# A two-layer vision network on one core: the layer-0 selective scan on 16 states x 8 channels, and attention with scores one key block ahead

## The chip, the cores and the metric

The kernel runs on one core of one Trainium2 chip. The metric is the device time of one execution in microseconds (us). Before the change it is 17,470.7 us, the median of three runs (17,456.07, 17,470.7 and 17,522.3).

The engines are named as in the profile: PE does the matrix products and loads their weights (PEld), DVE is the vector engine, ACT the scalar engine (activation functions), POOL the third elementwise engine; SP issues the transfers (DMA). SBUF is the on-chip memory, PSUM the accumulators that PE writes.

## The reference

Two images of 96 channels x 96 x 96 pass through two layers. Each layer adds a mixer to the image and then a two-layer feed-forward block (FFN), both after a normalisation over the channels.

The mixer of layer 0 projects to 192 channels, computes an offset per pixel, samples the image bilinearly there, and cuts the result into windows of 6 x 6 tokens. In each window it runs four selective scans (rows, columns, and both backwards; index kg), each over 192 channels with 16 states:

```python
def step(hst, inputs):
    ut, dt, bt, ct = inputs
    dA = jnp.exp(dt[..., None] * A)
    hst = hst * dA + (dt * ut)[..., None] * bt[:, :, None, :]
    y = jnp.einsum('bkdn,bkn->bkd', hst, ct)
    return (hst, y)
```

Here dt is the softplus of a projection, and B and C (bt, ct) are projections of the samples. The four results are added, normalised, gated and projected back to 96 channels.

The mixer of layer 1 is an attention of three heads with 32 channels each. Keys and values are the 9,216 pixels, queries are 2,304 cells, means of 2 x 2 pixels:

```python
attn = jnp.einsum('bhdn,bhdm->bhnm', k, q_samp) * scale
attn = jax.nn.softmax(attn, axis=-2)
distribution = jnp.einsum('bhdn,bhnm->bhdm', v, attn)
```

The distribution is then spread to the pixels with a local 3 x 3 softmax, a 5 x 5 depthwise convolution of the values is added, and the sum is projected.

## The kernel before, in words

**Layer 0** (`_layer0`, L581) goes through 32 stripes of 6 rows, that is 16 windows or 576 tokens each (T = 576, H2 = 288). For each stripe there is a front (`_l0_front`), a scan and a back (`_l0_back`).

The front normalises, projects (pi and pz), runs the 3 x 3 convolution pc on PE (L356), makes the offsets fr (L391), samples on POOL (L404 to L421), and then computes, for four directions and two halves of the channels, dl = softplus (eight units, L466 to L493) and du = dl times the samples xs. ACT, DVE and POOL each have a part of a unit: Abs, Relu, Exp and Ln on ACT, e on DVE (L485), the sums r, w and the product du on POOL (L488 to L491). dl and du are written to DRAM. At the places where a window begins, dl is set to 1e33, so that its decay becomes zero.

The scan puts 4 states x 32 channels into the 128 partitions. A section is one direction and one half of the channels. Per section, `load_section` brings dl and du from DRAM, each read four times over (864 KB each, the four copies leading). Per state group i of four, `decay` brings the row of C that is needed (cre, 288 KB) and computes dA = exp(A dl) on ACT (L636). Then there are two token halves, so 64 steps u a stripe:

- `b_rows` (L652): PE spreads the rows of B over the partitions by a product with a selection matrix, into PSUM (pB).
- `scan` (L668): DVE multiplies du by pB and puts the product bp into PSUM; L679: DVE scans h = dA h + bp over 864 columns, into SBUF; L680: POOL multiplies h by C.
- `states` (L694), three steps later: three products with 32 output columns each fold the states of h into py.

`collect` (L721 for one of the two cases) adds py to Y on DVE. The back normalises Y, gates and projects it and runs the FFN.

The order of the work is written out by hand: front and back are generators, whose `yield` states a price. Between two scan steps the loop takes generator steps of the back of the stripe before and of the front of the stripe after, until the sum of the prices has reached its share of `k.between` = 205. `_in_order` then fixes this order on PE, DVE, ACT and POOL.

**Layer 1** has, for each image: a normalisation stage; then `_l1_attention`; then the rows (`_l1_rows`) with the FFN. `_l1_attention` makes vT, kH and qH, then runs a max pass (L845, L852) that finds the maximum per query and head, so that it can be subtracted. Then comes the value pass: six chunks of 384 cells, and in each 72 key blocks of 128 pixels:

- scores sc: per head one bf16 product (L881) that puts in the negated maximum, and one fp32 product (L890);
- pr = exp(sc), one ACT instruction on 128 x 1152 (L898);
- values av (L900): four products with 33 output columns, two of 384 cells (heads 0 and 1, in one accumulator) and two of 192 cells (the halves of head 2, in another). The 33rd column of vT is one, so its row is the denominator.

The scheduler keeps the order of the code on PE: scores of a block, its values, scores of the next. At the end of a chunk, for each of the four parts, the denominator row is spread by a product (pb, L912), its reciprocal taken (L920) and multiplied in.

`_ln` (L77) is the normalisation that the nrm stage and all FFNs use: it takes the inverse square root with Ln and Exp on ACT (L97, L98).

Of the kernel before, what the change touches and what calls it, by code (L numbers as in the profile page):

```python
# [15 lines left out]
ENGINES = (  # L16
    mybir.EngineType.PE,
    mybir.EngineType.DVE,
    mybir.EngineType.Activation,
    mybir.EngineType.Pool,  # L20
)
# [3 lines left out]
NB = 2  # L25
# [10 lines left out]
NQ = 4  # L36
CB = 32
NBL = C // CB
PAST = 1e33
NG = 12  # L40
HID = 384
# [13 lines left out]
def _in_order(k, tc, start):  # L55

    last = {}
    for i in k.nc.cur_bb.bb.instructions[start:]:
        if i.engine in ENGINES:
            if i.engine in last:  # L60
                tc.add_manual_dep(
                    i,
                    last[i.engine].name,
                    mybir.DependencyInfo(
                        mybir.DependencyClass.NoSync, mybir.DependencyReason.DATA
                    ),
                    reason="in_order",
                )
            last[i.engine] = i


def _all(steps):
    for _ in steps:
        pass


def _ln(k, pool, psum, ptag, x, eps, out, pre, tags=None, bufs=None):  # L77
# [3 lines left out]
    t0, t1 = tags or (pre + "xc", pre + "sq")  # L81
# [3 lines left out]
    yield 1.3  # L85
    xc = pool.tile([C, 2, n], F32, tag=t0, name=pre + "xc", bufs=bufs)
    nc.vector.tensor_tensor(xc, x, mu[:C, :2, :n], ALU.subtract)
    sq = pool.tile([C, 2, n], F32, tag=t1, name=pre + "sq", bufs=bufs)
    nc.scalar.activation(sq, xc, AF.Square)
    yield 0.8  # L90
# [3 lines left out]
    yield 1.3  # L94

    rs = sq
    nc.scalar.activation(rs, va[:C, :2, :n], AF.Ln, bias=eps[:C])  # L97
    nc.scalar.activation(rs, rs, AF.Exp, scale=-0.5)  # L98
    yield 1.6
    kw = {"saturate": False} if out.dtype == F8 else {}  # L100
    nc.vector.tensor_tensor(out, xc, rs, ALU.mult, **kw)
    yield 0.7


def _ffn(k, pool, psum, ptag, w, x1, out, tags=None, bufs=None):
# [4 lines left out]
    yield from _ln(k, pool, psum, ptag, x1v, k.eps5, xq, "f", tags, bufs)  # L110
    h16 = pool.tile([128, NM, T], HP, tag="fh16", name="fh16")
    h8 = pool.tile([128, NM, T], F8, tag="fh8", name="fh8")
    for m in range(NM):
# [6 lines left out]
        yield 1.3  # L120
        nc.vector.tensor_scalar(
            h16[:, m, :], h16[:, m, :], w.b1[:, m : m + 1], 0.0, ALU.add, ALU.max
        )
    nc.vector.tensor_copy(h8, h16, saturate=False)
    yield 1
# [12 lines left out]
    yield 1.4  # L138
    nc.vector.tensor_scalar(y16, y16, w.b2, None, ALU.add)
    nc.vector.tensor_tensor(out, x1, y16, ALU.add)  # L140
    yield 0.9
# [28 lines left out]
def _l0_weights(k, a, cp, tmp, ps, dram):  # L170
# [33 lines left out]

    xp = tmp.tile([C, 2, KG, 6 + 2 * NS], F32, tag="xp", name="xp")
# [5 lines left out]
    k.w_bc = cp.tile([C, 2, 2, 3, 2, NS], F32, tag="w_bc", name="w_bc")  # L211
    for kg in range(KG):
        o, kk = kg % 2, kg // 2
        nc.vector.tensor_copy(k.w_dl[:, :, o, kk * 6 : kk * 6 + 6], xp[:, :, kg, 0:6])
        nc.sync.dma_start(k.w_dt[kk * 6 : kk * 6 + 6, kg, :], a["dt_w"][kg])
        for j in range(3):
            src = xp[:, :, kg, 6 : 6 + NS] if j < 2 else xp[:, :, kg, 6 + NS :]
            nc.vector.tensor_copy(k.w_bc[:, :, o, j, kk, :], src)


    k.selb = cp.tile([2 * CB, 2, NQ, 128], F32, tag="selb", name="selb")
    for j in range(2):
        rows = slice(CB * j, CB * j + CB)
        for kk in range(2):
            c0 = CB * j + NS * kk
            for i in range(NQ):
                nc.vector.tensor_copy(
                    k.selb[rows, kk, i].rearrange("p (q c) -> p q c", c=CB),
                    k.ident[rows, c0 + i : c0 + NS : NQ].unsqueeze(2).to_broadcast([CB, NQ, CB]),
                )  # L230


    k.fold = cp.tile([128, CB], F32, tag="fold", name="fold")
    nc.vector.tensor_reduce(
        k.fold, k.ident.rearrange("p (q c) -> p c q", c=CB), AX.X, ALU.add
    )

    ad = dram.tile([NS, KG * 2, C], F32, tag="ad", name="ad")
    src = a["A_logs"].rearrange("(n d) (k g) -> n d k g", n=NS, g=NG)
    for n in range(NS):
        nc.sync.dma_start(ad[n].rearrange("k (d g) -> d k g", g=NG), src[n])
    na = KG * 2 * NBL
    at = tmp.tile([NQ * na, 128], F32, tag="at", name="at")
    rows = ad.rearrange("(q i) k (b c) -> i (k b) q c", i=NQ, c=CB)
    for i in range(NQ):
        nc.sync.dma_start(
            at[i * na : (i + 1) * na, :].rearrange("p (q c) -> p q c", c=CB), rows[i]  # L250
        )
    pa = ps.tile([128, 128], F32, tag="pa", name="pa")
    nc.tensor.transpose(pa[:, : NQ * na], at, k.ident[: NQ * na, : NQ * na])
    k.A = cp.tile([128, NQ, KG, 2, NBL], F32, tag="A", name="A")
    Af = k.A.rearrange("p i k h b -> p (i k h b)")
    nc.scalar.activation(Af, pa[:, : NQ * na], AF.Exp)
    nc.vector.tensor_scalar(Af, Af, -1.0, -1e-30, ALU.mult, ALU.min)
# [9 lines left out]

def _l0_front(k, P, f, x, b, s):


    nc = k.nc
    r0 = WIN * s - 1
    lo, hi = max(r0, 0), min(r0 + 8, HW)
    temp = lambda shape, name: P.front.tile(shape, F32, tag="g", name=name, bufs=5)
    half2 = lambda v: v.rearrange("p (c n) -> p c n", c=2)


    xt = temp([C, 8, HW], "xt")
    if lo > r0:
        nc.gpsimd.memset(xt[:, 0, :], 0.0)  # L280
    if hi < r0 + 8:
        nc.gpsimd.memset(xt[:, 7, :], 0.0)
    nc.sync.dma_start(xt[:, lo - r0 : hi - r0, :], x[b, :, lo:hi, :])
    xin = P.front.tile([C, 2, 8, HW + 2], F32, tag="xin", name="xin")
    nc.gpsimd.memset(xin[:, :, :, 0 : HW + 2 : HW + 1], 0.0)
    yield 0.3

    halves = lambda v: v.rearrange("p (c r) w -> p c (r w)", c=2)
    mu = P.ps.tile(k.pshape, F32, tag="p", name="amu")
    for c in range(2):  # L290
        nc.tensor.matmul(mu[:C, c, :384], k.mean96, halves(xt)[:, c, :], start=True, stop=True)
    yield 1.7
    xc = temp([C, 2, 384], "axc")
    nc.vector.tensor_tensor(xc, halves(xt), mu[:C, :, :384], ALU.subtract)
    rs = temp([C, 2, 384], "ars")
    nc.scalar.activation(rs, xc, AF.Square)
    yield 1
    va = P.ps.tile(k.pshape, F32, tag="p", name="ava")
    for c in range(2):
        nc.tensor.matmul(va[:C, c, :384], k.mean96, rs[:, c, :], start=True, stop=True)  # L300
    yield 1.7
    nc.scalar.activation(rs, va[:C, :, :384], AF.Ln, bias=k.eps6[:C])
    nc.scalar.activation(rs, rs, AF.Exp, scale=-0.5)
    yield 1.8
    xn = temp([C, 8, HW], "xn")
    nc.gpsimd.tensor_tensor(halves(xn), xc, rs, ALU.mult)
    yield 1.7

    for half in range(2):
# [9 lines left out]
        yield 1.7  # L319
# [5 lines left out]
        yield 1  # L325
# [3 lines left out]
    for half in range(2):  # L329
# [9 lines left out]
        yield 1.3  # L339
# [5 lines left out]
        yield 1  # L345


    t = temp([C, 2, T], "t")
    for oh in range(2):
        pc = P.ps.tile(k.pshape, F32, tag="p", name="pc")  # L350
        n = 0
        for ih in range(2):
            for tap in range(9):
# [10 lines left out]
                yield 1.3  # L364
        nc.scalar.activation(  # L365
            half2(t[:, oh]),
# [5 lines left out]
        yield 0.8  # L372

    fr = temp([C, 2, WIN, HW], "fr")
    for yx in range(2):
# [10 lines left out]
        yield 2.6  # L386
# [3 lines left out]
        yield 0.8  # L390
    nc.vector.tensor_scalar(fr, fr, 0.5, 0.5, ALU.mult, ALU.add)  # L391
    yield 0.7

    xs0 = P.hand.tile([C, 2, T], F32, tag="xs0", name="xs0")
    xs1 = P.front.tile([C, 2, T], F32, tag="xs1", name="xs1")
    f.xs0 = xs0
    dif = temp([C, 2, 7, HW], "dif")
    top = temp([C, 2, WIN, HW], "top")
# [104 lines left out]
def _l0_back(k, P, f, ffn, res, dst):  # L503
# [74 lines left out]
    yield 0.1  # L578


def _layer0(k, tc, a, x, x2d):  # L581


    nc = k.nc
# [600 lines left out]
```

## Time and profile before

| | |
|---|---|
| profiled execution, its own time | 17,470.7 us |
| its span in the trace | 17,468.9 us |
| layer 0 | 0 to 10,720 us |
| image 1: normalisation, max pass, value pass, rows | 160, 644, 1,544, 971 us |
| image 2: normalisation, max pass, value pass, rows | 212, 639, 1,572, 1,007 us |
| busy over the span | PE 75%, DVE 55%, POOL 37%, ACT 36% |
| DMA | 929.26 MB, mean 53 GB/s |

The stages follow one another. Boundaries are read from the first and last instruction of each line; the first stage of image 1 begins at 10,720 us. In the profile a group of instructions is named by its line, its engine, what it writes and reads, and its size. A figure with x is a count. A trailing bracket is the time that the engine sat idle before the instruction, and who released it. Busy times do not tell by themselves what limits a stage: an engine that is idle may be waited for by nobody.

### The profile page before, as it was taken

How to read it: one execution, taken by the hardware profiler on the slowest of the kernel's cores; microseconds unless marked ns; L12 is line 12 of the kernel's file. 1: busy time of each engine (PE TensorE's matmuls, PEld its weight loads, DVE VectorE, ACT ScalarE, POOL GpSimd, SP SyncE). 2: the span in 40 equal slices, each digit the busy share in tenths (PEclk: the TensorE clock that was granted, in tenths of full speed). 3: DMA queues.
4: the chain of work that ended last, by engine and by line, in shares of the span. 5: the costliest groups of instructions: out<-in, count | busy, mean ns of one | idle time of the engine just before them, and what ended most of it. 6: DMA issues, size and time to landing. Idle time of an engine off the chain costs nothing.

```text
span 17468.9 us, 139858 instructions
## 1 busy us (share of the span) xinstructions
PE 13074.9 (75%) x52851; PEld 5578.3 (32%) x52851; DVE 9543.8 (55%) x7721; ACT 6238.1 (36%) x7697; POOL 6501.1 (37%) x4039
## 2 busy tenths in 40 slices
PE   6777777777777778777777776976668579766774
PEld 2233223223223223223223222222227332222463
DVE  3766666666666666666666665830006558000255
ACT  3444544544544444444444443013331120233211
POOL 4655655655655655655655652000001200000012
PEclk6556556556556556556556555579895555899756
DMA  1222222222222222222222221000000000000000
GB/s 59 93 84 80 91 86 81 89 88 81 87 88 81 86 91 80 84 94 80 84 93 80 83 91 48 0 1 1 1 3 7 8 10 0 1 1 1 3 8 7
DMA packets 292536, 929.26 MB, mean 53 GB/s; under 512 B 26300, under 2 KB 27060, under 8 KB 291764
## 3 DMA queue, kind: packets, MB, share of 16 engines
q1 hardware_dynamic: 291860, 920.31, 16.0%
q8 instruction: 416, 6.82, 0.2%
q14 instruction: 260, 2.13, 0.0%
HBM read 788.04 MB, written 132.17 MB: 53 GB/s over the span
## 4 chain that ended last, share of the span: by engine, by line
PE 48%; ACT 16%; DVE 12%; POOL 11%; issue 7%; DMA 5%; SPq 0%; ACTq 0%; POOLq 0%; DVEq 0%
PE pc L356 7%; PE pm L845 7%; PE av L900 6%; ACT pr L898 6%; PE pB L652 5%; PE sc L890 5%; PE py L694 4%; DVE h L679 4%; DMA cre<-c_d 4%; POOL h L680 3%; DVE acc L990 2%; ACT dA L636 2%; POOL acc L1018 2%; DVE bp L668 2%; PE lg L954 2%
## 5 line engine op out<-in xcount | busy, mean ns | idle before, releaser
L680 POOL TENSOR_TENSOR h<-h,cre 128x864 f32<-128x864 f32 x2048 | 4117.0, 2022 | 4136.9 <-DVE h L679 1502.6
L679 DVE TENSOR_TENSOR_SCAN h<-dA,bp 128x864 f32<-128x864 f32 x2048 | 4001.3, 1954 | 227.1 <-DVE bp L668 7.0
L668 DVE TENSOR_TENSOR bp<-dur,pB 128x864 f32<-128x864 f32 x2048 | 2169.9, 1060 | 2121.8 <-PE pB L652 1997.5
L636 ACT ACTIVATE dA<-dlr,A 128x576 f32<-128x576 f32 x3072 | 2154.3, 764 | 2590.0 <-DVE h L679 1800.9
L652 PE MATMUL pB<-bc,selb 32*128 32x288 f32 x4096 | 2440.7, 692 | 583.2 <-DVE bp L668 582.6
L694 PE MATMUL py<-h,fold 128*32 128x288 f32 x12288 | 2190.5, 627 | 771.1 <-DVE Y L721 339.9
L898 ACT ACTIVATE pr<-sc 128x1152 f32<-128x1152 f32 x864 | 976.4, 1130 | 3372.1 <-PE sc L890 3372.1
L900 PE MATMUL av<-pr,vT 128*33 128x384 f32 (+1 forms) x6912 | 1101.0, 443 | 940.7 <-ACT pr L898 940.7
L970 POOL MEMSET vch<- 96x1600 f32 x16 | 22.8, 1426 | 4482.7 <-PE av L900 2247.8
L652 PEld LDWEIGHTS pB<-bc,selb 32*128 32x128 f32 x4096 | 922.4, 279 | 2164.6 <-DVE bp L668 1092.8
L356 PE MATMUL pc<-xin,off 96*96 96x288 f32 x4608 | 1456.4, 472 | 95.1 <-ACT t L365 70.8
L920 DVE RECIPROCAL den<-pb 32x384 f32<-32x384 f32 (+1 forms) x48 | 93.6, 1951 | 2524.0 <-PE pb L912 2522.8
L845 PE MATMUL pm<-kH,qH 32*128 32x512 f32 x3888 | 1245.1, 1102 | 22.8 <-DVE m L852 21.3
L852 DVE TENSOR_REDUCE m<-pm 128x3 f32<-128x1536 f32 x648 | 1136.0, 1758 | 226.4 <-PE pm L845 204.3
L694 PEld LDWEIGHTS py<-h,fold 128*32 128x32 f32 x12288 | 381.4, 133 | 2158.5 <-issue 1370.8
L356 PEld LDWEIGHTS pc<-xin,off 96*96 96x96 f32 x4608 | 826.8, 188 | 734.1 <-issue 359.2
L1018 POOL TENSOR_TENSOR acc<-acc,ft 96x576 f32<-96x576 f32 x288 | 414.7, 1442 | 1474.6 <-DVE acc L990 1455.7
L890 PE MATMUL sc<-qH,kH 32*128 32x384 f32 x5184 | 946.9, 543 | 0.0
L900 PEld LDWEIGHTS av<-pr,vT 128*33 128x33 f32 x6912 | 347.5, 116 | 1862.3 <-ACT pr L898 1457.6
L1000 PE MATMUL pb<-ident,p 96*96 96x96 f32 x3456 | 415.7, 290 | 408.8 <-DVE ft L1010 394.0
L485 DVE SCALAR_TENSOR_TENSOR e<-dl,e 96x576 f32<-96x576 f32 x256 | 321.7, 1256 | 652.4 <-ACT dl L483 646.4
L845 PEld LDWEIGHTS pm<-kH,qH 32*128 32x128 f32 x3888 | 320.9, 298 | 945.0 <-DVE m L852 941.9
(201 smaller groups left out, 14182.9 us busy)
## 6 DMA issues: line engine op xcount, KB each, us to landing
cre<-c_d SPq DMA_DIRECT2D x1024, 288.0 KB
dlr<-dl_d SPq DMA_DIRECT2D x256, 864.0 KB
dur<-du_d SPq DMA_DIRECT2D x256, 864.0 KB
du_d<-du SPq DMA_DIRECT2D x384, 144.0 KB
dl_d<-dl SPq DMA_DIRECT2D x384, 144.0 KB
xt<-in_x SPq DMA_DIRECT2D x28, 288.0 KB
xr<-in_x SPq DMA_DIRECT2D x32, 216.0 KB
x2d<-x SPq DMA_DIRECT2D x32, 216.0 KB
```

Source lines behind the costliest of these rows:

```text
L356: nc.tensor.matmul(pc[:C, c, :H2], k.w_c1[:, ih, tap, oh * C : (oh + 1) * C], xin[:, ih, 3 * c + dy : 3 * c + dy + 3, dx : dx + HW], start ...
L636: nc.scalar.activation(dA[:, :, blk, :], rep[s][0][:, blk, :].rearrange("p (c n) -> p c n", c=2), AF.Exp, scale=k.A[:, i, o + 2 * kk, h, b ...
L652: nc.tensor.matmul(pB[:, :H2], k.selb[rows, kk, i, :], F[n].bc[o][rows, c * H2 : (c + 1) * H2], start=True, stop=True,)
L668: nc.vector.tensor_tensor(bv.rearrange("p (b n) -> p b n", b=NBL), rep[s][1][:, :, toks], brp.pop(u)[:, :H2].unsqueeze(1).to_broadcast([12 ...
L679: nc.vector.tensor_tensor_scan(hv, dv, bv, 0.0, ALU.mult, ALU.add)
L680: nc.gpsimd.tensor_tensor(h, h, cre[j][:, toks].unsqueeze(1).to_broadcast([128, NBL, H2]), ALU.mult)
L694: nc.tensor.matmul(P.py[CB * blk : CB * blk + CB, c, :H2], k.fold, ht[:, blk, :], start=(kk == 0 and i == 0), stop=(kk == 1 and i == NQ - 1),)
L845: nc.tensor.matmul(pm[:, hd, :], qH[hs, m * 128 : (m + 1) * 128], kH[hs, g * 512 : (g + 1) * 512], start=True, stop=True,)
L852: nc.vector.tensor_reduce(m18[:, :, g], pm, AX.X, ALU.max)
L890: nc.tensor.matmul(sc[:, hd, :384], kH[hs, n * 128 : (n + 1) * 128], qH[hs, cells], start=False, stop=True,)
L898: nc.scalar.activation(pr, sc[:, :, :384], AF.Exp, scale=HD**-0.5)
L900: nc.tensor.matmul(av[i][row : row + HD + 1, : hi - lo], vT[:, n, hd, :], pr[:, hd, lo:hi], start=(n == 0), stop=(n == nblk - 1),)
```

## The change

It has two parts that do not depend on each other, and one small thing that both share.

**Layer 0.** The 128 partitions hold 16 states x 8 channels. One step takes three groups of channels and all tokens, 128 x 1728. There are 32 steps a stripe. B and C are spread over the partitions by products with widened weights (pb), once per direction, and copied to SBUF (bc). dl and du are read from DRAM for every step, with 16 copies leading. dA is computed in place of the loaded dl, the product du B in place of the loaded du, the scan in the same place, the product with C too. A memset puts zero into dA where a window begins. Six products with a selection matrix (k.sel) fold a step into py. The sampling and the sums of the softplus are on DVE; r, w and e have one buffer each. Generators, prices and `_in_order` are gone from layer 0: the code calls scan, next front and back in turn, and the scheduler decides.

**Attention.** `scores` is called for the next block ahead of the values of the present one, also across chunks. pr has four buffers. The values of the three heads are three products with 32 output columns into one accumulator. The denominators are summed on DVE over the blocks (sums, 128 x 1152) and folded by three products at the end of a chunk, with one reciprocal. `_in_order` holds PE to this order.

**Shared.** `_ln` uses Sqrt on ACT and a reciprocal on DVE.

```diff
 def _ln(...)
...
-    nc.scalar.activation(rs, va[:C, :2, :n], AF.Ln, bias=eps[:C])
-    nc.scalar.activation(rs, rs, AF.Exp, scale=-0.5)
+    nc.scalar.activation(rs, va[:C, :2, :n], AF.Sqrt, bias=eps[:C])
+    nc.vector.reciprocal(rs, rs)
...
 def _l0_front(...)
...
-    g = nc.gpsimd
-    for half in range(2):
-        v = xin[:, half, 1:8, 1 : HW + 1]
-        g.tensor_tensor(dif[:, half], xin[:, half, 1:8, 2 : HW + 2], v, ALU.subtract)
...
+    nc.vector.tensor_tensor(dif, xin[:, :, 1:8, 2 : HW + 2], v, ALU.subtract)
+    nc.vector.tensor_tensor(top, dif[:, :, 0:6], fx, ALU.mult)
...
+                nc.scalar.activation(e, pt[:C, :, :H2], AF.Abs, bias=bias)
+                nc.scalar.activation(e, e, AF.Exp, scale=-1.0)
+                nc.vector.tensor_scalar(r, pt[:C, :, :H2], bias, 0.0, ALU.add, ALU.max)
+                nc.vector.tensor_scalar(w, e, 1.0, None, ALU.add)
+                nc.vector.scalar_tensor_tensor(e, w, 1.0, e, ALU.subtract, ALU.subtract)
+                nc.scalar.activation(w, w, AF.Ln)
+                nc.vector.tensor_tensor(w, w, e, ALU.subtract)
+                nc.vector.tensor_tensor(
+                    dl[:, half].rearrange("p (c n) -> p c n", c=2), w, r, ALU.add
+                )
+            nc.vector.tensor_tensor(du, dl, f.xs[o], ALU.mult)
...
+def _l0_scan(k, P, f):
...
+                for g0 in range(0, NG, U):
+                    dA = P.rep.tile([128, U, T], F32, tag="dA", name="dA", bufs=3)
+                    h = P.rep.tile([128, U, T], F32, tag="h", name="h", bufs=4)
+                    nc.sync.dma_start(
+                        dA.rearrange("p g t -> p (g t)"), _repeated(f.dl[kg], half, g0)
+                    )
+                    nc.sync.dma_start(
+                        h.rearrange("p g t -> p (g t)"), _repeated(f.du[kg], half, g0)
+                    )
+                    for g in range(U):
+                        i = (kg * 2 + half) * NG + g0 + g
+                        nc.scalar.activation(dA[:, g], dA[:, g], AF.Exp, scale=k.A[:, i : i + 1])
+
+                    first = 0 if kk == 0 else SEQ - 1
+                    nc.vector.memset(
+                        dA.rearrange("p g (w t) -> p (g w) t", t=SEQ)[:, :, first], 0.0
+                    )
+                    nc.vector.tensor_tensor(
+                        h, h, bc[kk][:, 0].unsqueeze(1).to_broadcast([128, U, T]), ALU.mult
+                    )
...
+                    nc.vector.tensor_tensor_scan(d1, d0, d1, 0.0, ALU.mult, ALU.add)
+                    nc.gpsimd.tensor_tensor(
+                        h, h, bc[kk][:, 1].unsqueeze(1).to_broadcast([128, U, T]), ALU.mult
+                    )
+                    for g in range(U):
+                        for c in range(2):
+                            nc.tensor.matmul(
+                                py[:C, c, :H2],
+                                k.sel[:, 11 - g0 - g : 11 - g0 - g + C],
+                                h[:, g, c * H2 : (c + 1) * H2],
...
 def _layer0(...)
...
+        ready = _l0_front(k, P, x, *stripes[0])
+        for n, (b, s) in enumerate(stripes):
+            f = ready
+            Y = _l0_scan(k, P, f)
+            if n + 1 < len(stripes):
+                ready = _l0_front(k, P, x, *stripes[n + 1])
+            _l0_back(k, P, f, Y, ffn, x2d[b, :, s * T : (s + 1) * T])
...
 def _l1_attention(...)
...
+        ahead = scores(0, 0)
         for mc in range(6):
...
+            av = pa.tile([128, 512], F32, tag="a", name="av")
+            sums = wk.tile([128, 3, 384], F32, tag="sums", name="sums", bufs=2)
             for n in range(nblk):
+                pr = ahead
+                if n + 1 < nblk:
+                    ahead = scores(mc, n + 1)
+                elif mc < 5:
+                    ahead = scores(mc + 1, 0)
                 for hd in range(HEADS):
                     nc.tensor.matmul(
+                        av[hd * HD : (hd + 1) * HD, :384],
                         vT[:, n, hd, :],
+                        pr[:, hd, :],
...
+                if n == 0:
+                    nc.vector.tensor_copy(sums, pr)
+                else:
+                    nc.vector.tensor_tensor(sums, sums, pr, ALU.add)
...
+        _in_order(k, tc, start, (mybir.EngineType.PE,))
```

## The prediction

> **What bounds the kernel now.** I read the page's totals first, then a table of stretches, then single lines and the order of time inside two stretches.
>
> ```profile
> PE 13074.9 (75%) x52851; PEld 5578.3 (32%) x52851; DVE 9543.8 (55%) x7721; ACT 6238.1 (36%) x7697; POOL 6501.1 (37%) x4039
> ```
>
> No engine is full over the whole span, so the stages must be read apart. Columns: stretch, its length, busy us of PE, PE weight load, DVE, ACT, POOL, then granted clock, DMA share, GB/s.
>
> ```profile
> 0.00:10720.00 10720.00, 8166.98 (x25733) 3191.14 (x25733) 7017.65 (x5140) 4799.05 (x6206) 6055.27 (x3729) 0.60 0.26 84
> 10880.00:11524.00 644.00, 625.65 (x1957) 161.90 (x1956) 570.79 (x344) 2.46 (x3) 0.00 (x0) 0.53 0.00 0
> 11524.00:13068.00 1544.00, 1043.96 (x7382) 397.33 (x7380) 48.01 (x40) 496.25 (x453) 0.00 (x0) 0.91 0.00 1
> 14890.00:16462.00 1572.00, 1069.26 (x7419) 407.46 (x7419) 60.09 (x52) 497.96 (x457) 1.43 (x1) 0.90 0.00 1
> ```
>
> Layer 0 is the first row: 10,720 of 17,469 us, PE 76% and DVE 65% busy. The last two rows are the value passes of the two images (the second row is a max pass, which the change leaves alone). In them PE is 68% and ACT 32% busy: 100% together, so they take turns. Instruction by instruction (start, length):
>
> ```profile
> 12391.86 1.17 PE L900 MATMUL av<-pr,vT 128*33 128x384 f32 x8 [1.11 <-ACT pr L898]
> 12392.95 0.58 PE L890 MATMUL sc<-qH,kH 32*128 32x384 f32 x1
> 12393.96 1.13 ACT L898 ACTIVATE pr<-sc 128x1152 f32<-128x1152 f32 x1 [2.15 <-PE sc L890]
> 12395.14 1.17 PE L900 MATMUL av<-pr,vT 128*33 128x384 f32 x8 [1.11 <-ACT pr L898]
> ```
>
> One key block is 12391.86 to 12395.14 = 3.28 us: value products 1.09, scores 1.0, exp 1.13, in series.
>
> In layer 0 the price of the scan matters. Its two DVE instructions (lowest/median/highest ns):
>
> ```profile
> L679 DVE TENSOR_TENSOR_SCAN h<-dA,bp x2048: 1952/1954/1956, 225.6 to 10670.9; 128x864 f32<-128x864 f32 x187
> L668 DVE TENSOR_TENSOR bp<-dur,pB x2048: 1045/1062/1064, 224.5 to 10669.7; 128x864 f32<-128x864 f32 x187
> ```
>
> First to last scan is 10,445 us for 32 stripes: 326.4 us each. Each of these two reads one input from PSUM, and neither ever gets longer, though POOL works beside them all the time. An operation with two SBUF inputs does (DVE, then POOL in the same microseconds):
>
> ```profile
> 5125.00 2.00 DVE L485 SCALAR_TENSOR_TENSOR e<-dl,e 96x576 f32<-96x576 f32 x1 [1.04 <-ACT dl L483]
> 5126.93 1.05 DVE L668 TENSOR_TENSOR bp<-dur,pB 128x864 f32<-128x864 f32 x1
> ```
> ```profile
> 5124.37 2.01 POOL L680 TENSOR_TENSOR h<-h,cre 128x864 f32<-128x864 f32 x1
> 5126.34 1.93 POOL L491 TENSOR_TENSOR du<-dl,xs 96x576 f32<-96x576 f32 x1
> ```
>
> L485 takes 0.73 us at its lowest; here it ends 0.62 after POOL's multiply ends at 5126.38. POOL's next, elsewhere 1.40, ends 1.27 after L485 does. They run one at a time, with about 0.13 us of start-up hidden at each handover.
>
> [...] while the 4-copy loads run alone (3115 to 3120 us) the share is 0.25 at 80 GB/s. [...]
>
> **The change, part 1: layer 0.** Per stripe 64 steps (multiply, scan, POOL multiply on 864 columns) become 32 on 1728. The states in partitions go from 4 to 16, so B no longer needs the 128 selection matmuls a stripe; multiply and scan now read both inputs from SBUF.
>
> Each loop step: [...] scan: 1954 ns for 864 is 2.08 ns per column beside 0.155 fixed, so 3.75; POOL multiply: 1.40 at 576 and 2.02 at 864 give 2.15 ns per column, so 3.88; a small memset 0.1. If the lock holds for whole instructions: 1.96 + 3.75 + 3.88 - 2 x 0.13 + 0.1 = 9.4 us. 32 steps are 300 us. DVE alone would be 5.8 (the bound below), and if the scan doesn't lock but the multiply does it is about 5.9. What else is there per step: ACT three exps of 0.76 = 2.3; PE 6 fold matmuls, 3 us at the rate of 0.5 each; DMA two loads of 864 KB, now 16 copies leading, thus all engines, at the 250 GB/s seen in the fullest stretches 7.1 us. All lie beneath 9.4.
>
> The hand interleave is gone. In the built order of the changed kernel, DVE has only the start of the next front (up to its first bilinear operations) between the scans; the rest stands after the last scan and before the next stripe's first multiply. That scan-free stretch, in series: five bilinear operations and two copies 13 us; pd, copy and first pt matmuls 7; eight softplus units, which pass ACT (Abs, Exp, Ln at 0.7 each, two table loads of 1.28), DVE and back, with single buffers: 4.4 to 9.4 us each, 61 in all with the back of the stripe between them; the FFN's tail 22; B and C spread by PE and the first copy 7. Sum 110 us. The same work costs nothing now because the scans of another section cover it. Bounds: 85 if units overlap, 140 if PE runs at half clock. SP's queue holds the store of x2 ahead of the fourth dA load, which joins the same end.
>
> So S = 300 + 110 = 410 us a stripe against 326 (385 to 440). Layer 0: 470 (front, then first loop) + 31 x 410 + 50 (last back, 47 now) = 13,230, against 10,720: +2,510.
>
> **Part 2: attention.** Scores of block n+1 stand ahead of the values of block n on PE (the built order confirms it, alternating), so exp is covered. PE per block: scores 0.75 to 0.85, and values as three strips of 384. Pairs of strips now stand 0.34 us apart, so a third beside them makes 0.7. With switches about 1.6. ACT needs 1.13 to 1.19, the new sum on DVE 1.36 (two SBUF inputs, POOL idle there: 0.00 busy). PE stays the bound. If the strips don't overlap it is 2.1; if everything is ideal 1.4. I take 1.6: 432 x 1.6 + 6 chunk ends of 5 = 723 us. The ends shrink too: one reciprocal of 384 (2.55) instead of four, with the next chunk's first scores already out. Saved: 1544 - 723 + 1572 - 723 = 1,670.
>
> **Part 3: normalisations.** Ln and Exp become Sqrt and a DVE reciprocal: fewer table loads (1.28 each), 3.75 us more DVE per 576 columns. In the nrm and row stages that trades within 60 us either way; I take 0, the rows hiding it under PE and POOL.
>
> Sum, against the profiled execution's 17,470.7 (span 17,468.9; it is also the median of the three runs): 17,471 + 2,510 - 1,670 = **18,310 us**, 4.8% slower.
>
> **Rivals.**
> (a) Faster: [...] POOL slips in between. For it: no row shows a scan with two SBUF inputs. Against: L485. Then DMA sets the step at 7.1 us: S = 227 + 110 = 337, layer 0 = 397 + 31 x 337 + 50 = 10,890, total 15,975. It decides from S = 383: there layer 0 costs 470 + 31 x 383 + 50 = 12,390, 1,670 more than now, which is just what attention gives; that is a step below 8.5 us with the stretch at 110.
> (b) The clock. The max pass, PE 97% busy, is granted 0.53; the value passes now, 68% busy, 0.91. A denser value pass may sink too, to 3.1 us a block: saving 410 in place of 1,670, total 19,570. For it: 10 blocks after each chunk boundary now take 4.99 us. Against: 385 of 432 run at full clock with PE mostly occupied.
> (c) The scan-free stretch is covered more than the built order tells, engines running ahead of DVE: 70 us, S = 370, layer 0 11,990, total 17,070.
> That the attention doesn't do what it says is ruled out by the built order.
>
> **Chances.** Forecast 0.72 (its own range, S from 385 to 440: 17,535 to 19,240; 0.05 of it falls within 0.5%), (a) 0.10, (b) 0.10, (c) 0.08. About 0.5% is what a measurement of this kernel can tell from no change. Faster 0.18, same 0.05, slower 0.77. The range takes in (b) and (c) and leaves (a) out: 17,050 to 19,600.
>
> **What would show it.** Right: the scan's median between 3.75 and 7.6 us with POOL and DVE never both inside a locked pair; steps of 9.4 us; a stretch of about 110 us per stripe without a scan; blocks of 1.6 us in the value passes. Wrong: scans of 3.75 under a running POOL multiply; steps of 7 us with the DMA share near 1; blocks of 3 us at a clock near 0.5; gaps well off 110.

## The result, and the profile after

The changed kernel takes 18,214.7 us (median of three, 18,213.0 to 18,218.8) against 17,470.7: 1.0419 times as long, 95% interval 1.0386 to 1.0452. The forecast was 18,310. Both parts have the sign that was forecast, and both came out smaller than forecast.

| | before | after | difference | forecast |
|---|---|---|---|---|
| layer 0, to the first normalisation of layer 1 | 10,718 | 12,837 | +2,119 | +2,510 |
| value passes, first fp32 score to last value product | 1,542.7 + 1,557.3 | 843.5 + 842.7 | -1,414 | -1,670 |
| normalisation stages | 113.5 + 112.8 | 133.3 + 132.6 | +40 | 0 |
| all else | | | +3 | 0 |
| span | 17,468.9 | 18,217.0 | +748 | +840 |

The totals of the profile after:

```profile
PE 12366.3 (68%) x48538; PEld 6723.8 (37%) x48538; DVE 15218.6 (84%) x9106; ACT 5687.9 (31%) x7013; POOL 5994.2 (33%) x1444
```

DVE went from 55% to 84% busy. Part of that is waiting inside an instruction, as the two lines of the scan loop show (lowest/median/highest ns):

```profile
L458 DVE TENSOR_TENSOR h<-h,bc x1024: 1895/1903/5607, 134.3 to 12776.1; 128x1728 f32<-128x1728 f32 x171
L465 DVE TENSOR_TENSOR_SCAN h<-dA,h x1024: 3691/7257/7285, 136.8 to 12778.0; 128x1728 f32<-128x1728 f32 x171
```

A scan that takes 3.7 us at its lowest takes 7.26 at the median. One step in time, DVE and then POOL:

```profile
5031.72 1.90 DVE L458 TENSOR_TENSOR h<-h,bc 128x1728 f32<-128x1728 f32 x1
5033.65 7.26 DVE L465 TENSOR_TENSOR_SCAN h<-dA,h 128x1728 f32<-128x1728 f32 x1
5040.89 1.90 DVE L458 TENSOR_TENSOR h<-h,bc 128x1728 f32<-128x1728 f32 x1
```
```profile
5031.90 5.39 POOL L466 TENSOR_TENSOR h<-h,bc 128x1728 f32<-128x1728 f32 x1 [4.65 <-DVE dA L455]
5041.08 5.39 POOL L466 TENSOR_TENSOR h<-h,bc 128x1728 f32<-128x1728 f32 x1 [3.79 <-DVE dA L455]
```

POOL's multiply is issued at 5031.90, while DVE's multiply runs to 5033.62. It ends at 5037.29, 3.67 us after that. The scan, issued at 5033.65, ends at 5040.91, 3.62 us after POOL. So the three stand one after the other: 9.17 us from one L458 to the next. The median over all steps is 9.18 us, the mean 9.37. The lock of the prediction and the expectations is a name for this: DVE's and POOL's instructions with two SBUF inputs run one at a time, as these times show it.

Stages of the kernel after (columns as before: stretch, length, busy PE, PE load, DVE, ACT, POOL, clock, DMA share, GB/s; the clock is what PE was granted, 1.00 being full speed): most of one scan loop, the stretch without scan behind it, and of the value pass of image 1 the first chunk and the other five.

```profile
5012.00:5229.30 217.30, 147.17 (x452) 88.14 (x452) 212.15 (x79) 61.20 (x83) 119.52 (x23) 0.82 0.75 171
5229.30:5329.40 100.10, 46.71 (x116) 24.95 (x117) 63.25 (x75) 51.96 (x62) 7.65 (x4) 0.61 0.40 103
13660.70:13888.00 227.30, 227.28 (x1084) 60.99 (x1087) 97.17 (x72) 81.79 (x73) 0.00 (x0) 0.50 0.00 1
13891.00:14502.10 611.10, 610.42 (x5403) 188.07 (x5400) 497.02 (x368) 405.99 (x362) 0.00 (x0) 1.00 0.01 1
```

In the loop DVE is 98% busy, waiting inside its instructions included. In the stretch behind it no engine is full: they wait for each other, and DVE has 63 us of work in 100. In the value pass PE never stops, yet chunk 1 has a clock of 0.50 throughout and the rest 1.00. A block at full clock, with the exp now beneath PE's work (an fp32 product counts as two passes, so x6 is three products):

```profile
13895.16 0.85 PE L730 MATMUL av<-pr,vT 128*32 128x384 f32 x6
13895.29 1.13 ACT L715 ACTIVATE pr<-sc 128x1152 f32<-128x1152 f32 x1 [0.56 <-PE sc L707]
13895.94 0.34 PE L698 MATMUL sc<-sh,onesb 2*128 2x384 bf16 x3
13896.11 0.81 PE L707 MATMUL sc<-qH,kH 32*128 32x384 f32 x6
13896.85 0.85 PE L730 MATMUL av<-pr,vT 128*32 128x384 f32 x6
```

From one av to the next it is 1.69 us; in chunk 1 the same block takes 3.15.

Three theories were left for the runs: that DVE and POOL taking turns (and not transfers or DVE's own work) set the step of the scan; that the stretch between the loops is waiting rather than work; and that the clock of chunk 1 depends on what PE has been doing, not on time.

### The profile page after: what moved, and what is told of

Same layout as the page of the kernel before. It is cut to its first block, busy times and chain, and to the rows that moved or that the text cites. A ratio compares the mean times of both kernels' runs of the same rounds, so it can differ in the third digit from the quotient of the medians.

```text
span 18217.0 us, 128521 instructions
## 1 busy us (share of the span) xinstructions
PE 12366.3 (68%) x48538; PEld 6723.8 (37%) x48538; DVE 15218.6 (84%) x9106; ACT 5687.9 (31%) x7013; POOL 5994.2 (33%) x1444
## 4 chain that ended last, share of the span: by engine, by line
DVE 29%; PE 28%; issue 24%; ACT 7%; POOL 7%; DMA 3%; SPq 0%; DVEq 0%; POOLq 0%; ACTq 0%
DVE h L465 10%; DVE h L458 9%; PE pm L664 6%; POOL h L466 5%; PE av L730 4%; PE py L471 4%; PE sc L707 4%; DVE acc L823 2%; POOL acc L851 2%; DMA h<-du_d 2%; PE lg L787 2%; PE sc L698 1%; DMA dA<-dl_d 1%; ACT L390 1%; DVE frs L79 1%
## 5 line engine op out<-in xcount | busy, mean ns | idle before, releaser
L466 POOL TENSOR_TENSOR h<-h,bc 128x1728 f32<-128x1728 f32 x1024 | 5452.7, 5327 | 6748.7 <-DVE h L465 4046.3
L471 PE MATMUL py<-h,sel 128*96 128x288 f32 x12288 | 4600.6, 543 | 3395.5 <-POOL h L466 3278.0
L465 DVE TENSOR_TENSOR_SCAN h<-dA,h 128x1728 f32<-128x1728 f32 x1024 | 6393.4, 6246 | 27.6
L471 PEld LDWEIGHTS py<-h,sel 128*96 128x96 f32 x12288 | 2604.9, 220 | 5346.5 <-POOL h L466 3773.6
L452 ACT ACTIVATE dA<-dA,A 128x576 f32<-128x576 f32 x3072 | 2160.9, 765 | 3990.7 <-DMA dA<-dl_d 3968.4
L458 DVE TENSOR_TENSOR h<-h,bc 128x1728 f32<-128x1728 f32 x1024 | 2387.0, 2336 | 70.8 <-ACT bc L434 70.8
L740 DVE TENSOR_TENSOR sums<-sums,pr 128x1152 f32<-128x1152 f32 x852 | 1157.1, 1358 | 476.7 <-ACT pr L715 472.9
L730 PE MATMUL av<-pr,vT 128*32 128x384 f32 x5184 | 825.3, 556 | 0.9 <-ACT pr L715 0.9
L427 PE MATMUL pb<-xs,w_bc 96*128 96x288 f32 x2048 | 578.6, 437 | 6.8 <-DVE r L386 4.6
L787 PEld LDWEIGHTS lg<-ones,pr 96*96 96x96 f32 x3456 | 549.8, 270 | 44.9 <-DVE p L794 19.4
```

Source lines behind the costliest of these rows:

```text
L452: nc.scalar.activation(dA[:, g], dA[:, g], AF.Exp, scale=k.A[:, i : i + 1])
L458: nc.vector.tensor_tensor(h, h, bc[kk][:, 0].unsqueeze(1).to_broadcast([128, U, T]), ALU.mult)
L465: nc.vector.tensor_tensor_scan(d1, d0, d1, 0.0, ALU.mult, ALU.add)
L466: nc.gpsimd.tensor_tensor(h, h, bc[kk][:, 1].unsqueeze(1).to_broadcast([128, U, T]), ALU.mult)
L471: nc.tensor.matmul(py[:C, c, :H2], k.sel[:, 11 - g0 - g : 11 - g0 - g + C], h[:, g, c * H2 : (c + 1) * H2], start=(n == 0), stop=(n == last),)
L730: nc.tensor.matmul(av[hd * HD : (hd + 1) * HD, :384], vT[:, n, hd, :], pr[:, hd, :], start=(n == 0), stop=(n == nblk - 1),)
```

## The experiments

**Attention by itself.** The kernel before, with the new `_l1_attention` in place of the old one, its order on PE included; `_ln` and layer 0 stay.

```diff
-def _in_order(k, tc, start):
+def _in_order(k, tc, start, engines):
...
-        _in_order(k, tc, start)
+        _in_order(k, tc, start, ENGINES)
...
+        _in_order(k, tc, start, (mybir.EngineType.PE,))
```

> The kernel before with only the new attention function; layer 0 and the normalisations as before. Theory (the parts are independent and the attention gains 699 + 715 us, as the two stages of the changed kernel show): 17,471 - 1,414 = 16,057 us, within 30. If the forecast's 1,670 had been right but for layer 0: 15,800. Rival (the slow first chunk of 72 blocks at 3.15 us comes from what layer 0 left behind, or from the new normalisation): blocks of 1.69 us from the start here, about 15,850.

Measured: 16,054.1 us (four runs), 0.9188 of before, which took 17,480.9 beside it (0.9171 to 0.9205). The parts add: 17,470.7 - 1,414 = 16,057. The first chunk of both images again has 71 blocks of 3.15 us, so neither layer 0 nor the new normalisation makes them.

**Without the multiply by C.**

```diff
-                    nc.gpsimd.tensor_tensor(
-                        h, h, bc[kk][:, 1].unsqueeze(1).to_broadcast([128, U, T]), ALU.mult
-                    )
```

> The changed kernel without POOL's multiply by C: the states go into the fold unweighted (that part of the computation is left out). Lock theory: the scan's median falls from 7.26 to 3.76 us, and the step from 9.18 us to whatever is next, the transfers at about 7.1 us or DVE at 1.90 + 3.76 + 0.10 = 5.8; total near 18,215 - 1,024 x 2.1 = 16,060 (14,750 if DVE sets it). Rival (loads or the fold set the step, and the long scan only fills the time): step stays above 8.5 us, total above 17,500.

Measured: 16,382.9 us in one run. The scan's line and, from the groups, the wait of the multiply ahead of it:

```profile
L465 DVE TENSOR_TENSOR_SCAN h<-dA,h x1024: 3687/3757/3760, 136.8 to 10842.8; 128x1728 f32<-128x1728 f32 x171
```
```profile
L458 DVE TENSOR_TENSOR h<-h,bc 128x1728 f32<-128x1728 f32 x1024 | 1993.3, 1952 | 1131.8 <-DMA h<-du_d 1053.4 <-ACT bc L434 76.6 <-PE py L468 0.9
```

The scan never takes more than 3.76 us once POOL is silent. The step is now 7.35 us in the mean (9.37 with POOL), and what DVE waits for is the transfer of du. So the forecast's floor of 7.1 us by DMA was close, and it was not what set 9.18. (That 16 leading copies keep all DMA engines busy was the author's estimate. In the changed kernel, from 10,847.2 to 10,855 us, where such loads run alone, the DMA share reads 1.01 at 248 GB/s, against 0.25 at 80 for four copies before.) (The total is above the 16,060 expected: the step is 0.27 us longer than taken, and image 2 had a second chunk of 3.15 us blocks, some 104 us; more on this below.)

**The same work with the product in PSUM.**

```diff
-                    nc.vector.tensor_tensor(
-                        h, h, bc[kk][:, 0].unsqueeze(1).to_broadcast([128, U, T]), ALU.mult
-                    )
...
+                    for g in range(U):
+                        bp = P.ps.tile([128, 1024], F32, tag="b", name="bp", bufs=1)
+                        bv = bp[:, :T]
+                        nc.vector.tensor_tensor(bv, h[:, g], bc[kk][:, 0], ALU.mult)
...
+                        nc.vector.tensor_tensor_scan(hv, dv, bv, 0.0, ALU.mult, ALU.add)
```

> The changed kernel, same work, but B's product goes to PSUM in three pieces of 576 and each piece is scanned from there, so that the scan has one SBUF input; the working PSUM pool has two buffers in place of three. Lock theory: the scan never waits for POOL; a piece of scan takes about 1.35 us at every run, DVE 3 x (0.76 + 1.35) + 0.1 = 6.4 us a step, POOL and the multiplies in turn 3.6 + 2.3 = 5.9, so the transfers set the step at about 7.1: near 16,100, up to 16,400 if the stretch without scan grows by the missing buffer. Rival (POOL's multiply delays by memory traffic or by order[...]): the scans of 576 stretch as well and the step stays near 9.2, 18,200.

Measured: 18,669.1 us in one run: the total was wrong. The scan does what the theory says, 1,283 to 1,355 ns in all 3,072 pieces, beside POOL too. DVE, then POOL:

```profile
5156.18 0.77 DVE L461 TENSOR_TENSOR bp<-h,bc 128x576 f32<-128x576 f32 x1
5157.07 1.35 DVE L465 TENSOR_TENSOR_SCAN h<-dA,bp 128x576 f32<-128x576 f32 x1
5158.46 2.77 DVE L461 TENSOR_TENSOR bp<-h,bc 128x576 f32<-128x576 f32 x1
5161.27 1.35 DVE L465 TENSOR_TENSOR_SCAN h<-dA,bp 128x576 f32<-128x576 f32 x1
```
```profile
5156.37 4.25 POOL L466 TENSOR_TENSOR h<-h,bc 128x1728 f32<-128x1728 f32 x1 [4.43 <-DVE h L465]
```

By these times POOL's multiply makes its way from 5156.95, where DVE's multiply ends, to 5160.62. One piece of scan passes beside it in its usual 1.35 us. The instruction behind it in DVE's queue is a multiply with two SBUF inputs, and it takes 2.77 us in place of 0.77, so it waits 2.0. The expectation added up what each engine has to do and forgot the order of DVE's queue: the next piece of scan could have run beside POOL, but it stands behind this multiply and starts at 5161.27, when the multiply has ended (5161.23). The step is 8.7 us, the loop 287 us in place of 294, and the stretch without scan grew from 104 to 126. I didn't separate the missing PSUM buffer from the scheduler's new order there.

**C on DVE.**

```diff
-                    nc.gpsimd.tensor_tensor(
+                    nc.vector.tensor_tensor(
                         h, h, bc[kk][:, 1].unsqueeze(1).to_broadcast([128, U, T]), ALU.mult
                     )
```

> The changed kernel with the multiply by C moved from POOL to DVE, nothing else. Lock theory: DVE 1.90 + 3.76 + 1.90 + 0.10 = 7.7 us a step without any wait, less than 9.18: total near 18,215 - 1,024 x 1.5 = 16,680. Rival (no lock; DVE's own work sets the step): 9.18 + 1.90 = 11.1 us a step, 20,160.

Measured: 18,617.3 us in one run: the total was wrong, the step right. The step is 7.64 us, as the lock theory said (7.7), and the loop falls from 294 to 245 us; the rival's 11.1 is out. But the stretch without scan grew from 104 to 168 us: the scheduler set the projections and the convolution of the next front, which ran beside the loop, behind it. 31 x 64 us lost, 32 x 49 gained. The step is settled by this run; the total is that of another schedule, and the last run takes it up.

**Back and front in the scan loop.** Front and back as generators, taken between the steps:

```diff
+                    u += 1
+                    while steps and (done < 175.0 * (u - 1) / 28 or u >= 29):
+                        try:
+                            done += next(steps[0])
+                        except StopIteration:
+                            steps.pop(0)
```

> The changed kernel with the back of the stripe before and the front of the stripe after written between the 32 steps of the scan (generators again, prices by guess; the order on the engines stays the scheduler's). Theory (the stretch without a scan is a series of waits between ACT, DVE and PE around 63 us of DVE work): it vanishes but for this DVE work, S = 294 + 63 = 357 us or a little less in place of 399, total about 18,215 - 31 x 42 = 16,900. Rival (the work costs the same wherever it stands, since DVE waits in order for ACT): S stays near 395, 18,100.

Measured: 17,609.7 us in one run; S, the time from stripe to stripe, is 378.6 us. The stretch shrinks from 104 to 10 us; the loop grows from 294 to 368, by 74 rather than 63. So waiting was part of the stretch, but less than thought: 20 us of 104 come back, not 42. Over one stripe:

```profile
5000.00:5378.60 378.60, 243.05 (x724) 146.48 (x724) 340.07 (x177) 138.58 (x179) 169.07 (x36) 0.78 0.70 161
5152.19 3.92 DVE L115 TENSOR_SCALAR fy<-fy,f0b2g 96x576 f16<-96x576 f16 x1
```

DVE still idles 38 us, and an operation like L115, 0.36 us in the stretch where POOL is idle, takes 3.92 beside POOL's multiply (POOL 5150.56 to 5155.95).

**Scores ahead only.** The kernel before, with PE held in order over the pass; values as before (four products of 33 output columns, one of them the column of ones).

```diff
+        ahead = scores(0, 0)
...
-                sc = ps.tile([128, 3, 512], F32, tag="s", name="sc")
...
-                nc.scalar.activation(pr, sc[:, :, :384], AF.Exp, scale=HD**-0.5)
+                pr = ahead
+                if n + 1 < nblk:
+                    ahead = scores(mc, n + 1)
+                elif mc < 5:
+                    ahead = scores(mc + 1, 0)
```

> The kernel before with scores one block ahead and PE held to that order; values as before (four products of 33 columns, the ones column, reciprocals as before). Theory (before, PE and ACT took turns: 2.15 us of PE and 1.13 of ACT a block): PE sets the block, about 2.1 us at full clock; 864 x 1.18 = 1,020 us less if the clock holds, some 200 to 300 less than that if the first chunk stays at half clock: 16,450 to 16,750. Rival (the exp was hidden already, or the clock falls to half throughout): blocks of 3.3 us and more, 17,400 to 17,900.

Measured: 16,258.3 us in one run; 2.01 us a block from block 2 of chunk 1 on. This part alone brings 1,215 us (the kernel before took 17,473.4 beside it), where the whole attention brings 1,414. It is more than expected: besides the exp, the kernel before loses 88 blocks of some 5 us at half clock, which are gone too. And no chunk stays at half clock here, unlike chunk 1 of the whole change.

**Strips and sums only.** The new attention without running ahead. "Strips" are the value products of the three heads, 32 output columns each, side by side:

```diff
-                pr = ahead
-                if n + 1 < nblk:
-                    ahead = scores(mc, n + 1)
-                elif mc < 5:
-                    ahead = scores(mc + 1, 0)
+                pr = scores(mc, n)
```

> The kernel before with values in three strips, denominators summed on DVE and one reciprocal a chunk, but each block's scores still after the values of the block before. Theory: PE and ACT go on taking turns; a block loses only what the strips save, 1.09 - 0.70 = 0.39 us: 2.9 us; 864 x 0.39 + 10 chunk ends x 10 us = 440 us less: 17,030. Rival (the strips alone bring most of it): blocks near 2 us, 16,300.

Measured: 18,230.9 us in one run, slower than before. A block takes 4.46 us, not 2.9: the clock is 0.51 over the whole pass (0.91 before). This half of the change, made alone, loses.

**A burst in chunk 1.** Attention alone, and behind the values of one block:

```diff
+                if mc == 0 and n == at_block:
+                    bst = pa.tile([128, 512], F32, tag="a", name="bst")
+                    for hd in range(HEADS):
+                        nc.tensor.matmul(
+                            bst[hd * HD : (hd + 1) * HD, :384],
+                            k.ones,
+                            pr[:, hd, :],
...
```

> The kernel before with the new attention, and six products more (three heads, ones x pr, into an accumulator that nobody reads) right after the values of one block of the first chunk: block 3 in image 1, block 30 in image 2. This is what stands at each chunk's end (av, then den: twelve products over 128 rows in a row). Theory (the clock is granted after a long enough run of full-row products, and the pattern of the loop keeps it but doesn't win it): the blocks fall from 3.15 to 1.69 us right there, saving 67 x 1.46 = 98 us in image 1 and 41 x 1.46 = 60 us in image 2: 16,054 - 158 = 15,896. Rival (the clock rises after some 230 us of dense work, or with the change of chunk itself): both images keep 71 blocks of 3.15 us, 16,056.

Measured: 15,980.3 us in one run, between the two. In image 1 the blocks fall from 3.15 to 1.69 us right behind the burst, at block 5. In image 2 the same burst at block 30 changes nothing, and the blocks stay at 3.15 us to the end of the chunk. Neither theory holds as put: it isn't time and it isn't the change of chunk, but a run of twelve passes (2.78 us at half clock) does not always do. The run without C shows the same of the natural one: at the end of its first chunk in image 2 the clock stayed, and rose one chunk later.

The trace tells the two bursts apart. Its clock changes only on a grid with steps of 3.413 us. First image 1, then image 2: the values and the burst, and the step of the grid that holds the longer part of them, with the step behind it.

```profile
11573.24 1.50 PE L912 MATMUL av<-pr,vT 128*32 128x384 f32 x6
11574.52 1.50 PE L922 MATMUL bst<-pr,ones 128*32 128x384 f32 x6
14224.73 1.50 PE L912 MATMUL av<-pr,vT 128*32 128x384 f32 x6
14226.01 1.50 PE L922 MATMUL bst<-pr,ones 128*32 128x384 f32 x6
```
```profile
11574.10:11577.52 3.42, 3.42 (x19) 0.83 (x12) 1.36 (x1) 0.40 (x1) 0.00 (x0) 0.50 0.00 0
11577.52:11580.93 3.41, 3.41 (x33) 1.05 (x30) 1.68 (x2) 2.26 (x2) 0.00 (x0) 1.00 0.00 0
14222.85:14226.26 3.41, 3.41 (x21) 1.21 (x21) 1.59 (x2) 1.13 (x1) 0.00 (x0) 0.50 0.00 0
14226.26:14229.67 3.41, 3.41 (x18) 0.83 (x15) 1.12 (x1) 0.38 (x1) 0.00 (x0) 0.50 0.00 0
```

In image 1 the grid leaves 1.92 us of the 2.78 in one step, and the next step has the full clock. In image 2 it cuts them into 1.53 and 1.25 (1.77 in either step with the values of the blocks beside them), and nothing changes.

**A longer burst.** 18 products (36 passes) behind block 1 of both images.

```diff
-                if mc == 0 and n == at_block:
+                if mc == 0 and n == 1:
                     bst = pa.tile([128, 512], F32, tag="a", name="bst")
-                    for hd in range(HEADS):
+                    for r in range(6):
+                        for hd in range(HEADS):
```

> The kernel before with the new attention, and 18 products more (36 passes, about 7.7 us at half clock, unread) after the values of block 1 of each image's first chunk. Theory (a long enough run of full-row products wins the clock, the shorter one does so only where it falls well; the loop then keeps it): blocks of 1.69 us from block 3 on in both images, 16,054 - 2 x (69 x 1.46 - 6) = 15,865. Rival (the clock comes by chance or by time): one image or both stay at 3.15 us through chunk 1, 15,960 or 16,070.

Measured: 15,865.3 us (five runs), 0.9067 of before (0.9054 to 0.9080). This is the expected total; in both images the blocks take 1.69 us from there on.

**The same ahead of the max pass.** The same six rounds stand there too, over vT in place of pr:

```diff
+        bst = pa.tile([128, 512], F32, tag="a", name="bst")
+        for r in range(6):
+            for hd in range(HEADS):
...
+                    vT[:, 0:4].rearrange("p n h d -> p (n h d)"),
...
         mxall = big.tile(
```

> The same, with 18 such products also ahead of each max pass. If 32-row products keep a clock that is won: PE falls to about 1.0 us a group, DVE's reduce of 1.76 us sets it, 324 x 0.19 = 60 us less an image: 15,750. If they don't keep it: the max pass stays at 634 us but for the first groups, 15,880.

Measured: 15,898.7 us in one run; the max passes took 629 and 639 us. Around the first:

```profile
10920.00:10930.00 10.00, 10.00 (x54) 3.99 (x52) 0.00 (x0) 5.10 (x4) 0.00 (x0) 1.00 0.01 2
10930.00:10960.00 30.00, 20.50 (x114) 5.59 (x108) 28.44 (x18) 0.00 (x0) 0.00 (x0) 1.00 0.00 0
10960.00:11560.00 600.00, 588.11 (x1836) 151.27 (x1836) 539.99 (x324) 0.00 (x0) 0.00 (x0) 0.53 0.00 0
```

The clock is full when the pass begins; it was so without this burst as well (1.00 from 10,890 to 10,910 us in the run of the longer burst). DVE at once becomes the bound (28.4 of 30 us), PE is 68% busy with 32-row products, and the clock is lost for the rest of the pass: after 64 us here and 6 in image 2, after 33 and 35 without this burst. So winning it does next to nothing here.

**Strips and sums with the burst.** The two edits above together.

> Strips and sums without scores ahead (18,231 us, 4.46 us a block, half clock throughout), with the burst after block 1. If the loop keeps a clock that is won: about 2.9 us a block, 18,231 - 860 x 1.5 = 16,940. If taking turns with ACT loses it: back to 4.46 within a few blocks, 18,240.

Measured: 18,216.1 us in one run, 4.46 us a block. Behind the burst:

```profile
11555.00:11565.00 10.00, 7.51 (x56) 2.00 (x48) 2.61 (x2) 2.26 (x2) 0.00 (x0) 0.84 0.00 0
11565.00:11575.00 10.00, 7.50 (x39) 2.31 (x39) 2.83 (x3) 2.26 (x2) 0.00 (x0) 0.50 0.00 1
```

Within some 10 us the clock is lost. With scores ahead the same products keep it for the rest of the pass.

**Everything that helped in layer 0.** The changed kernel with three edits from above: back and front in the loop, the multiply by C on DVE, and the longer burst.

> The changed kernel with back and front in the scan loop (378.6 us a stripe, 17,610), the multiply by C on DVE, and the burst in attention. Lock theory (POOL's 3.6 us stand in the series of locked work, the same on DVE 1.9): 32 x 1.54 = 49 us less a stripe, S = 330: 17,610 - 1,520 - 190 = 15,900. Rival (no lock; DVE is the bound and gets 61 us more): S = 440, 19,300.

Measured: 15,663.7 us (four runs), 0.8950 of before (0.8938 to 0.8962), the fastest version here and faster than both kernels. S falls from 378.6 to 323.4:

```profile
5000.00:5323.40 323.40, 221.82 (x722) 136.34 (x722) 310.35 (x209) 142.21 (x182) 8.49 (x4) 0.83 0.82 188
```

DVE has 61 us more to do than with POOL's help, and a stripe is 55 us shorter. With front and back placed alike in both, the series of DVE and POOL is shown in the total too. Layer 0 now takes 10,478 us, 240 less than in the kernel before: the new layout of the scan is no loss in itself. What made it slower was POOL's part in the series and the stretch without a scan.

## Why the prediction was right

- **The step of the scan** was forecast at 9.4 us and is 9.18 in the median: multiply 1.90 (forecast 1.96), scan 3.76 (3.75), POOL 3.82 at its lowest (3.88), the handovers hiding some 0.3 (0.26), and the memset (0.10 us, from 5031.73) lying under the multiply (from 5031.72). The 1.96 us for the multiply is the author's estimate; 755 ns for 576 elements (L101) and 1,350 for 1,152 (L523) in the trace before give 1.95 for 1,728. The split of 1954 ns for 864 columns into 2.08 ns a column and 0.155 us fixed is an estimate too, which one size alone can't tell; 3.76 us for 1728 columns (the run without C) and 1.35 for 576 (the product in PSUM) give 2.09 and 0.15. That the three stand in series is shown by the trace and by two runs (no C: 3.76 us scans; C on DVE: 7.64 us steps). Rival (a) is out; this is the series as it was predicted.
- **The stretch without a scan** was forecast at 110 us and is 104. That it is there at all was read from the built order. But "the same work costs nothing now" is more than was shown: put back between the steps it still cost 84 us a stripe.
- **S** is 398.7 us, not 410, the front before the first scan 137, not 170, the last loop 288, not 300: together 31 x 11.3 + 33 + 12 = 395 us that layer 0 is shorter than forecast. The terms were 2 to 6% too large, the first front 24%.
- **Attention** was forecast at 1,670 us saved and saved 1,414. The term that was mis-sized is "432 x 1.6": at full clock a block is 1.69, the values 0.78 rather than 0.7 and the scores 0.91 rather than 0.75 to 0.85 (2 x 355 x 0.09 = 64 us), and 71 blocks an image ran at 3.15 (2 x 71 x 1.55 = 220). Chunk ends cost less than the 5 us taken, which gives some 40 back. The 1,544 and 1,572 us of before were stretches wider than the passes (1,542.7 and 1,557.3), which makes another 16. Rival (b), the clock, was no case of its own: it came true for one chunk in six. The forecast gave it for the whole pass or not at all. Its reason for it was misread as well: the kernel before lost 1 to 11 blocks at the start of a chunk to half clock, not 10 each time.
- **The normalisations** were put at 0 and cost 40 us: in the two stages with nothing else to do, the reciprocal of 3.75 us stands in the chain. All that is left, the rows among it, changed by 3 us.
- **Two slips of the sums**: 432 x 1.6 + 6 x 5 is 721 us, not 723, and 432 blocks of 3.1 us with the same ends save 380, not rival (b)'s 410. The first moves the forecast by 4 us, the second not at all.

So the total, 95 us off, is better than its parts: -391, +256 and +43 partly cancel, and that is luck. What was right on its merits is the series of DVE and POOL, the stretch without a scan, and the exp covered by PE.

## What to carry to other kernels

Before moving an elementwise operand from PSUM to SBUF on one of two engines that work side by side, look in the trace for instructions that get longer beside the other engine's (here a scan of 7.26 us in place of 3.76). Where there are some, add up both engines' work as one series; then giving the second engine's part to the first can be faster than sharing (here steps of 7.64 us in place of 9.18). Look at each half of a change by itself: scores ahead alone gave 1,215 us, strips alone lost 760, and together they gave 1,414. And when PE is dense but its clock reads 0.5, try some microseconds of wasted products over all 128 rows at the start of the stage, enough of them to fill a whole step of the clock's grid wherever they fall (here 36 passes behind block 1 of each image, against steps of 3.413 us: 189 us less in all).

## What the runs showed of the hardware that was not expected

- PE can be 100% busy for 227 us and be granted a clock of 0.50 (the changed kernel from 13,660.7 to 13,888 us). Here dense work was not enough. In chunk 1 six passes over 128 rows alternate with nine over 32 or 2. Twelve full-row passes in a row, as at a chunk's end, raised the clock 14 times and missed twice in the versions with strips and scores ahead; 36 raised it all eight times that they stood in a value pass.
- The granted clock changes only on a grid of 3.413 us (to within 0.02 us in every trace here: 278 stretches of full clock or half in the trace of the kernel before, 1,546 in that of the changed kernel). In the value passes of the eleven versions with scores ahead there are 969 steps of it at half clock with PE busy throughout. After 32 the next step had full clock, after 937 it did not. The work over 128 rows (values, denominators, bursts) in the step was 1.77 us or more in all of the 32, and 1.77 or less in all of the 937. In the trace of the changed kernel they are 134: 2.22 and 2.37 us in the two with full clock behind them, 1.77 at most in the other 132. So it seems to be the place of the twelve passes in the grid that decides: the fourteen that raised the clock brought at least 1.83 us into a step, the two that missed at most 1.77. The margin is thin, and the ends of PE's instructions in a trace are modelled. All this was read from the traces afterwards; no run shifted the passes to test it.
- By the same reading it is the strips that hold chunk 1 at half clock. Three strips take 1.50 us in a block of 3.15 and never bring more than 1.77 into one step. The four products of 33 columns in "scores ahead only" took 2.13 us at half clock, brought 2.04 and 1.94 us into the first full step, and had the full clock in the next:

```profile
11553.06 2.13 PE L909 MATMUL av<-pr,vT 128*33 128x384 f32 x8
11556.05 1.17 PE L909 MATMUL av<-pr,vT 128*33 128x384 f32 x8
```

- Once won, the clock stayed at 1.00 under the same mix for 611 us, but was lost within some 10 us in the strips without scores ahead (PE 75% busy) and within 6 to 64 us in the max pass (68% busy, 32-row products). The strips without scores ahead won it at 16 of their 20 chunk ends and lost it again each time; up to 2.13 us of full-row work in a step missed there, with PE idle in part of the step. So full-row time is not all that counts, and what sets the loss stays open.
- A scan with two SBUF inputs waits for POOL (7.26 against 3.76 us) just as a multiply does (2.77 against 0.77 for 576 columns), and one with an input in PSUM doesn't (1,283 to 1,355 ns).
